# Adding four scan directions and centring them with matmuls, and a grouped convolution over moved copies, in a four-layer vision kernel on one core

## The chip, the core and the metric

The kernel runs on one core of one Trainium2 chip. Five engines work side by side, each through its own instruction queue in order: PE (TensorE, matrix multiplication into PSUM), DVE (VectorE), ACT (ScalarE), POOL (GpSimd) and SP (SyncE, which here issues nearly all DMA transfers). The metric is the device time of one execution in microseconds (us), as the median of several runs. A profile is one further execution with every instruction recorded.

## What is computed

The input is 4 images of 96 channels, 64 by 64. Four layers follow one another, each as x + layer(group_norm(x)): an attention layer (layer 0), a selective scan over four directions with a gated convolution block (layer 1), a 3x3 convolution (layer 2) and a second selective scan with more blocks (layer 3). Two pieces of it matter here. In both scan layers the results of four directions are added and normalised over 192 channels:

```python
# layer 1 (layer 3 has the same with its own names)
ys = (y1 + y2 + y3 + y4).reshape(Bs, E, Hs, Ws)      # E = 192; y3, y4 are transposed in h and w
yn = jnp.moveaxis(ys, 1, -1)
mu = yn.mean(-1, keepdims=True)
var = yn.var(-1, keepdims=True)
yn = (yn - mu) / jnp.sqrt(var + 1e-05) * ln_g + ln_b
```

Layer 3 ends in a block with a grouped 3x3 convolution and a 1x1 convolution of the same 24 channels:

```python
up = conv2d(x[:, :uc], s1)                            # 48 -> 24 channels
low = conv2d(x[:, uc:], s2)
Y1 = conv2d(up, gw, gb, groups=2) + conv2d(up, p1)    # 24 -> 96 channels
Y2 = jnp.concatenate([conv2d(low, p2), low], 1)
```

## The kernel before

The heavy part is eight selective scans: layers 1 and 3 for each of the four images. A scan is cut into 384 units; one unit takes a tile of 128 partitions (16 states times 8 channels) by 1024 positions. For a unit, SP fetches rep (the step sizes, repeated), ACT takes its exponential (L1786), PE spreads the driving term into bx with two bf16 matmuls over 24 rows, DVE multiplies bx by B (L1800) and runs the scan instruction (hs, L1807), POOL multiplies by C (rep, times_c, L1819), and for every third unit PE adds up the states of three units in acc. rep is fetched four units ahead, bx is made two units ahead.

Everything else is written as Python generators, the stages "first" (group norm, layer 0, and the input projection and depthwise convolution of layer 1), "second" (the end of layer 1, layer 2 and the beginning of layer 3) and "third" (the end of layer 3). The program order is written out by hand: scan 0 is accompanied by first(1), scans 1 and 2 by second(0) and second(1), scans 3 and 4 by first(2) and first(3), scans 5 and 6 by second(2) and second(3), and scan 7 by third(0), third(1) and third(2), one after the other. Before scan 0, first(0) runs with nothing beside it; after scan 7, third(3) does (here called the tail).

How much of a stage goes beside a unit is a budget, in slots of about one matmul of 512 columns: each unit gets PACE, less 2.1 in every third unit (where the sums in acc stand), and at most half a slot is carried over. In a unit at most two slots begin, the second one only while more than 0.9 of the budget is left. When a scan nears its end (unit 365), what is left of the stage is run at once.

```python
PACE = 3.5
...
if at == 0:
    work, owed = Slots(beside(s)), 0.0
...
if at == per - NG - LEAD - 1:
    work.run()
owed = min(owed, 0.5) + PACE - (2.1 if i % 3 == 1 else 0.0)
```

second and third begin with directions. For each half h of the 192 channels it loads the row-wise sum (y_row) into V and the column-wise sum (y_col) into yc, of which there is one buffer, and POOL adds yc, read across its rows, to V in eight blocks of 512 (L1370). layer_norm follows: per block, two matmuls with a constant 1/192 form the mean, DVE subtracts it from both halves (L1138), ACT squares the result (L1140), and a matmul with one column set adds the squares into one row of the bank acc. Then come a square root, a reciprocal, and a matmul that spreads each row again.

In third, squeeze makes up (24 channels, padded to 66 by 66) and low (24 channels). The grouped convolution then runs per block of 512 positions as nine matmuls over the 24 rows of up, one for each tap, and a tenth with the 1x1 weights (conv with more); an eleventh, over low, makes Y2. All matmuls go through one helper, line L948 of the profile.

Of the kernel before, what the change touches and what calls it, by code (L numbers as in the profile page):

```python
# [9 lines left out]
F32 = mybir.dt.float32  # L10
# [13 lines left out]
PADW = 66  # L24
# [869 lines left out]
def streams(ctx: ExitStack, tc: tile.TileContext, x, wts, cst, out, wat, cat, flag):  # L894
# [14 lines left out]
    ct = keep.tile([128, n0 + n2 - n1], F32, name="ct")  # L909
    cols = keep.tile([128, 5], F32, name="cols")  # L910
    nc.scalar.dma_start(out=ct[:, :n0], in_=cst[:, :n0])
# [3 lines left out]
    def wv(name, rows=None):  # L915
        return _view(wt, wat[name], rows)
# [16 lines left out]
    addn = cv("addn")  # L933
    for j, v in enumerate((GN_EPS, 1.0, -1.0, 1.0 / 96.0, 1.0 / 192.0)):
# [9 lines left out]
    def img(t):  # L944
        return t.rearrange("p (a b) -> p a b", b=W)
# [134 lines left out]

    def conv(o, weight, src, j, k=3, more=()):


        n = k * k
        taps = [(weight[:, t, :], src[:, 8 * j + t // k : 8 * j + t // k + 8, t % k : t % k + W]) for t in range(n)]
        taps.extend(more)
# [34 lines left out]
    def layer_norm(pool, V, n, gains, each):  # L1121
# [25 lines left out]
        add(7)  # L1147
        yield
        r = pool.tile([8, PCH], F32, name="ln_r", bufs=1)
        nc.scalar.activation(r, acc[:8], AF.Sqrt, bias=eps[:8])  # L1150
# [207 lines left out]
    def directions(pool, b):  # L1358

        V = pool.tile([96, 2, L], F32, name="V", bufs=1)  # L1360
        with tc.tile_pool(name="dirs", bufs=1) as T:
            for h in range(2):
                t = T.tile([96, W, H], F32, name="yc")
                for j in range(4):
                    nc.sync.dma_start(out=t.rearrange("p a b -> p (a b)")[:, bass.ts(j, CH)],
                                      in_=y_col[h][b][:, bass.ts(j, CH)])
                    nc.sync.dma_start(out=V[:, h, bass.ts(j, CH)], in_=y_row[h][b][:, bass.ts(j, CH)])
                for j in range(8):
                    v = img(V[:, h, bass.ts(j, PCH)])
                    nc.gpsimd.tensor_tensor(v, v, t[:, :, 8 * j : 8 * j + 8].rearrange("p a b -> p b a"), ALU.add)  # L1370
# [170 lines left out]
    def finish(PX, b, V):  # L1541
        with tc.tile_pool(name="p3", bufs=2) as pool:
# [15 lines left out]

            yield from layer_norm(pool, V, 2, wv("l3_ss_outn_g"), gate)
            for j in range(8):  # L1560
# [9 lines left out]
        with tc.tile_pool(name="p4", bufs=2) as pool:  # L1570
            up = pool.tile([24, PADW, PADW], F32, name="up", bufs=1)
            border(up, 1)
            low = pool.tile([24, L], F32, name="low", bufs=1)

            def squeeze(j):
                js = bass.ts(j, PCH)
                v = V[:, 0, js]
                nc.scalar.activation(v, v, AF.Identity, bias=wv("l3_ln_b"))
                yield 0.5
                for m, o in enumerate((inner(up, j), img(low[:, js]))):  # L1580
                    q = bank()
# [6 lines left out]
            w = staged(pool, "l3_gwc", "l3_pwc1", "l3_y2", "l3_fin")  # L1588

            sums = pool.tile([96, 2, 8], F32, name="csums", bufs=1)  # L1590
            for j in range(8):
                js = bass.ts(j, PCH)
                p = bank()
                yield from conv(p[:96], w["l3_gwc"][:24], up, j, more=[(w["l3_pwc1"][:24], inner(up, j))])
                nc.scalar.activation(V[:, 0, js], p[:96], AF.Identity, bias=wv("l3_gwc_b"),
                                     accum_out=sums[:, 0, j : j + 1])
                yield 1
                q = bank()
                mm(q[:96], w["l3_y2"][:24], low[:, js])
                yield  # L1600
                nc.scalar.activation(V[:, 1, js], q[:96], AF.Identity, accum_out=sums[:, 1, j : j + 1])
                yield 1
# [258 lines left out]
    store, waiting = [], []  # L1861

# [88 lines left out]
    with tc.manual_schedule():  # L1951
# [83 lines left out]
```

## Time and profile before

| | |
|---|---|
| time, median of 3 runs | 15360.42 us (15356.96 to 15373.58) |
| the profiled execution, its own time | 15373.82 us |
| its span, first to last instruction | 15371.9 us |
| PE busy | 12696.9 us, 83% |
| PE's mean granted clock | 0.799 |
| DVE busy | 11681.2 us, 76% |
| POOL busy | 10373.1 us, 67% |
| ACT busy | 8329.7 us, 54% |
| DMA moved | 2645.47 MB, 172 GB/s over the span |

The profile gives for each group of instructions the busy time, the mean duration of one and the idle time of its engine just before them, with what ended it. Matmuls are pipelined: a record's own duration can be longer than the distance to the next record, so the cost of one in a dense row is the group's busy time over its count. A float32 matmul leaves two records. A tile called one, bx, acc or held is in PSUM; "one" is what a stage works in beside a scan, and the same matmuls stand under "bx" where a stage runs alone.

### The profile page before, as it was taken

What the parts mean: (1) busy time and instruction counts of PE and PEld (TensorE: products, weight loads), DVE (VectorE), ACT (ScalarE), POOL (GpSimd) and SP (SyncE); (2) the same over time, 40 slices, a digit from 0 to 9 for tenths busy, and PEclk for the clock granted to TensorE, in tenths of its full rate; (3) what the DMA queues carried; (4) which work ended last, traced back from release to release, by engine and by line L of the source; (5) the groups of instructions that cost most, each with busy time, mean ns of one, the idle gap of its engine ahead of it and who ended that gap; (6) DMA issues with size and microseconds to landing.
All of it is one profiled execution on the core that took longest, in us unless ns stands there. A gap on an engine that the chain in (4) does not pass through costs nothing.

```text
span 15371.9 us, 128027 instructions
## 1 busy us (share of the span) xinstructions
PE 12696.9 (83%) x41106; PEld 3467.9 (23%) x41106; DVE 11681.2 (76%) x7516; ACT 8329.7 (54%) x11647; POOL 10373.1 (67%) x4722
## 2 busy tenths in 40 slices
PE   8978986988879797888788985988789796868778
PEld 2322221222212121222122221222222121211112
DVE  0067888887879888779877888888888787767771
ACT  3155565556745575555655564656645575444531
POOL 0056777777868677678866877877778676656660
PEclk9977886888879787879778886988889786666655
DMA  0066788786878787768866787787878687666660
GB/s 8 26 155 161 187 201 203 188 202 173 218 175 203 178 201 194 170 165 200 218 156 165 189 205 196 194 199 177 213 179 205 171 208 182 158 156 159 163 157 24
DMA packets 901883, 2645.47 MB, mean 172 GB/s; under 512 B 106640, under 2 KB 256752, under 8 KB 901200
## 3 DMA queue, kind: packets, MB, share of 16 engines
q1 hardware_dynamic: 900544, 2635.94, 69.2%
q8 instruction: 326, 5.34, 0.2%
q14 instruction: 357, 2.92, 0.1%
q10 hardware_dynamic: 656, 1.27, 0.0%
HBM read 2170.18 MB, written 466.62 MB: 172 GB/s over the span
## 4 chain that ended last, share of the span: by engine, by line
PE 48%; DVE 19%; DMA 8%; POOL 7%; ACT 7%; issue 6%; SPq 1%; DVEq 0%; POOLq 0%; another core or an unknown queue 0%; ACTq 0%
PE one L948 30%; DVE hs L1807 13%; PE acc L948 8%; PE bx L948 8%; DVE bx L1800 4%; DMA rep<-dd 4%; POOL rep L1819 4%; PE held L948 2%; ACT rep L1786 2%; POOL V L1370 1%; ACT L1786 1%; ACT ex L1233 1%; DMA yc<-ycol 1%; POOL delta L1731 0%; ACT delta L1726 0%
## 5 line engine op out<-in xcount | busy, mean ns | idle before, releaser
L1819 POOL TENSOR_TENSOR rep<-hs,bc 128x1024 f32<-128x1024 f32 x3072 | 7234.2, 2359 | 3398.4 <-DVE hs L1807 2906.3
L1807 DVE TENSOR_TENSOR_SCAN hs<-rep,carry,bx 128x1024 f32<-128x1024 f32 x2304 | 5401.4, 2344 | 335.6 <-POOL rep L1819 75.4
L1800 DVE TENSOR_TENSOR bx<-bx,bc 128x1024 f32<-128x1024 f32 x3072 | 3721.5, 1211 | 1197.8 <-PE bx L948 1097.4
L1786 ACT ACTIVATE rep<-rep,l_decay 128x1024 f32<-128x1024 f32 x3072 | 3495.8, 1143 | 818.3 <-DMA rep<-dd 790.6
L948 PE MATMUL bx<-parts,spread 24*128 24x512 bf16 x6144 | 1433.7, 438 | 1709.5 <-DVE hs L1807 1662.9
L948 PE MATMUL acc<-rep,ct 128*32 128x512 f32 x12288 | 2628.7, 739 | 165.9 <-POOL rep L1819 165.8
L1807 DVE TENSOR_TENSOR_SCAN hs<-rep,bx 128x1024 f32<-128x1024 f32 x768 | 1754.4, 2284 | 237.1 <-POOL rep L1819 153.2
L948 PEld LDWEIGHTS <-spread 24*128 24x128 bf16 x6144 | 314.2, 93 | 4199.2 <-DVE hs L1807 2774.5
L948 PE MATMUL one<-band,dg 96*96 96x512 f32 x2304 | 1117.1, 620 | 0.0
L948 PE MATMUL one<-upad,diag 96*96 96x512 f32 x2016 | 1033.1, 649 | 4.0 <-ACT ur L1113 2.7
L948 PEld LDWEIGHTS acc<-rep,ct 128*32 128x32 f32 x12288 | 508.7, 127 | 1993.6 <-issue 1513.4
L948 PE MATMUL one<-qq,kk 96*128 96x512 f32 x1152 | 826.6, 807 | 132.4 <-ACT ex L1233 79.0
L1233 ACT ACTIVATE ex<-one 128x512 f32<-128x512 f32 x576 | 343.0, 595 | 758.6 <-PE one L948 753.8
L1786 ACT ACT_TABLE_LOAD x500 | 641.5, 1283 | 96.6 <-DMA rep<-dd 88.4
L948 PE MATMUL one<-pr,ct 6*96 6x512 f32 x1024 | 649.2, 729 | 37.6 <-ACT pr L1691 6.2
L948 PE MATMUL one<-hp,diag 96*96 96x512 f32 x1152 | 618.9, 676 | 51.9 <-POOL diag L1073 51.9
L1815 ACT COPY carry<-hs 128x1 f32<-128x1 f32 x2304 | 408.8, 177 | 398.6 <-DVE hs L1807 395.9
L948 PE MATMUL one<-vpad,diag 96*96 96x512 f32 x1200 | 598.6, 635 | 0.0
L948 PE MATMUL held<-ex,cols 128*32 128x256 f32 x3072 | 571.8, 453 | 12.0 <-ACT ex L1233 6.0
L948 PE MATMUL held<-ex,vT 128*32 128x256 f32 x3072 | 572.3, 453 | 0.0
L948 PEld LDWEIGHTS one<-band,dg 96*96 96x96 f32 x2304 | 350.0, 166 | 531.3 <-issue 515.7
L948 PEld LDWEIGHTS one<-upad,diag 96*96 96x96 f32 x2016 | 321.4, 174 | 500.7 <-issue 483.6
(3395 smaller groups left out, 14517.9 us busy)
## 6 DMA issues: line engine op xcount, KB each, us to landing
rep<-dd SPq DMA_DIRECT2D x3072, 512.0 KB
parts<-du SPq DMA_DIRECT2D x1024, 144.0 KB
bc<-rows SPq DMA_DIRECT2D x256, 512.0 KB
dd<-delta SPq DMA_DIRECT2D x256, 384.0 KB
du<-cut SPq DMA_DIRECT2D x256, 384.0 KB
us<-urow SPq DMA_DIRECT2D x128, 384.0 KB
du<-cut SPq DMA_DIRECT2D x256, 192.0 KB
yrow<-yo SPq DMA_DIRECT2D x128, 384.0 KB
```

Source lines behind the costliest of these rows:

```text
L948: nc.tensor.matmul(o, lhsT=lhsT, rhs=rhs, start=first, stop=last)
L1233: nc.scalar.activation(last.rearrange("p a b -> p (a b)"), p, AF.Exp, scale=HD**-0.5)
L1370: nc.gpsimd.tensor_tensor(v, v, t[:, :, 8 * j : 8 * j + 8].rearrange("p a b -> p b a"), ALU.add)
L1786: nc.scalar.activation(a, a, AF.Exp, scale=decay[tag][:, k, NG * h + m : NG * h + m + 1])
L1800: nc.vector.tensor_mul(bx, bx, ready[i // NG][2][:, 0, :])
L1807: nc.vector.tensor_tensor_scan(out=hs, data0=a, data1=bx, initial=carry[:, h, m : m + 1] if c else 0.0, op0=ALU.mult, op1=ALU.add)
L1815: nc.scalar.copy(carry[:, h, m : m + 1], live[i][1][:, CH - 1 : CH])
L1819: nc.gpsimd.tensor_tensor(a, hs, ready[i // NG][2][:, 1, :], ALU.mult)
```

## The change

Three things are changed.

- The sum and the centring. directions loads both halves of yc before it begins (two buffers) and y_row in blocks of 512, one block ahead. For each block and half, four matmuls add up in one bank: the two parts of the same half with the matrix centre, and the two parts of the other half with a constant -1/192. The yc parts are read across rows, at a stride of 64 elements. ACT copies the bank to V. centred takes the place of layer_norm's first part and only squares and adds; scaled is layer_norm's second part, unchanged.
- The grouped convolution. up becomes 96 partitions by 66 by 64: three copies of the 24 channels at partitions 0, 32 and 64, moved by one column each. The weights stand beneath one another in gw, the 1x1 weights are added to the middle tap by POOL, and three matmuls over 96 rows take the place of ten over 24. sq3 makes the three copies in one matmul, and ACT writes them in three parts.
- The order. PACE is 3.65, and a stage begins at unit 2 of its scan, not at unit 0.

```diff
-    def conv(o, weight, src, j, k=3, more=()):
+    def conv(o, weight, src, j, k=3):
...
+    minus_mean = cols[:, 5:6].to_broadcast([128, 96])
+    centre = keep.tile([96, 96], F32, name="centre")
+    nc.vector.tensor_scalar(centre, ident[:96, :96], 1.0 / 192.0, None, ALU.subtract)
...
+    def centred(pool, V, gains, each):
+        acc = held()
+        sq = []
+        def add(last):
+            k, t = sq.pop()
+            mm(acc[:8], cv("means")[:96, 1, 7 - k // 2 : 15 - k // 2], t, k == 0, last)
+        for k in range(16):
+            if sq:
+                add(False)
+                yield
+            t = pool.tile([96, PCH], F32, name="ln_sq", bufs=2)
+            nc.scalar.activation(t, V[:, k % 2, bass.ts(k // 2, PCH)], AF.Square)
+            sq.append((k, t))
+            yield 0
+        add(True)
+        yield
+        yield from scaled(pool, V, 2, gains, each, acc)
...
     def directions(pool, b):
         V = pool.tile([96, 2, L], F32, name="V", bufs=1)
         with tc.tile_pool(name="dirs", bufs=1) as T:
+            yc = [T.tile([96, W, H], F32, name=f"yc{h}") for h in range(2)]
+            def rows(j):
+                t = T.tile([96, 2, PCH], F32, name="yr", bufs=2)
+                for h in range(2):
+                    nc.sync.dma_start(out=t[:, h, :], in_=y_row[h][b][:, bass.ts(j, PCH)])
+                return t
+            yr = rows(0)
             for h in range(2):
-                t = T.tile([96, W, H], F32, name="yc")
                 for j in range(4):
-                    nc.sync.dma_start(out=t.rearrange("p a b -> p (a b)")[:, bass.ts(j, CH)],
+                    nc.sync.dma_start(out=yc[h].rearrange("p a b -> p (a b)")[:, bass.ts(j, CH)],
                                       in_=y_col[h][b][:, bass.ts(j, CH)])
-                    nc.sync.dma_start(out=V[:, h, bass.ts(j, CH)], in_=y_row[h][b][:, bass.ts(j, CH)])
-                for j in range(8):
-                    v = img(V[:, h, bass.ts(j, PCH)])
-                    nc.gpsimd.tensor_tensor(v, v, t[:, :, 8 * j : 8 * j + 8].rearrange("p a b -> p b a"), ALU.add)
+            for j in range(8):
+                ahead = rows(j + 1) if j < 7 else None
+                for h in range(2):
+                    p = bank()
+                    parts = [(m, v) for k, m in ((h, centre[:96]), (1 - h, minus_mean[:96])) for v in
+                             (img(yr[:, k, :]), yc[k][:, :, 8 * j : 8 * j + 8].rearrange("p a b -> p b a"))]
+                    for t, (m, v) in enumerate(parts):
+                        mm(p[:96], m, v, t == 0, t == 3)
+                        if t < 3:
+                            yield (1,)
+                    yield
+                    nc.scalar.copy(V[:, h, bass.ts(j, PCH)], p[:96])
                     yield 1
+                yr = ahead
...
-                yield from layer_norm(pool, V, 2, wv("l1_ln_g"), gate)
+                yield from centred(pool, V, wv("l1_ln_g"), gate)
...
-            up = pool.tile([24, PADW, PADW], F32, name="up", bufs=1)
-            border(up, 1)
+            up = pool.tile([96, PADW, W], F32, name="up", bufs=1)
+            for s in (up[:, 0, :], up[:, PADW - 1, :], up[0:32, :, 0:1], up[64:96, :, W - 1 : W]):
+                nc.gpsimd.memset(s, 0.0)
+            sq3 = pool.tile([96, 3, 32], F32, name="sq3", bufs=1)
+            nc.gpsimd.memset(sq3, 0.0)
+            gw = pool.tile([96, 3, C], F32, name="gw", bufs=1)
+            nc.gpsimd.memset(gw, 0.0)
+            pw = pool.tile([96, C], F32, name="pw", bufs=1)
+            n, m, _ = wat["l3_gwc"]
+            for s in range(3):
+                nc.gpsimd.tensor_copy(sq3[:, s, 0:24], wv("l3_sq")[:, 0, :])
+                nc.sync.dma_start(out=gw[32 * s : 32 * s + 24],
+                                  in_=wts[:24, n : n + m].rearrange("p (a b c) -> p a b c", a=3, b=3)[:, :, s, :])
+            n, m, _ = wat["l3_pwc1"]
+            nc.sync.dma_start(out=pw[32:56], in_=wts[:24, n : n + m])
+            nc.gpsimd.tensor_tensor(gw[32:56, 1, :], gw[32:56, 1, :], pw[32:56], ALU.add)
...
-                for m, o in enumerate((inner(up, j), img(low[:, js]))):
-                    q = bank()
-                    mm(q[:24], wv("l3_sq")[:, m, :], v)
-                    yield
-                    nc.scalar.copy(o, img(q[:24]))
-                    yield 1
+                q = bank()
+                mm(q[:96], sq3.rearrange("p a b -> p (a b)"), v)
+                yield
+                for s in range(3):
+                    a, n = max(1 - s, 0), W - abs(1 - s)
+                    nc.scalar.copy(up[bass.ts(s, 32), 1 + 8 * j : 9 + 8 * j, a : a + n],
+                                   img(q[bass.ts(s, 32)])[:, :, a + s - 1 : a + s - 1 + n])
+                yield 1
+                q = bank()
+                mm(q[:24], wv("l3_sq")[:, 1, :], v)
+                yield
+                nc.scalar.copy(low[:, js], q[:24])
+                yield 1
...
-                yield from conv(p[:96], w["l3_gwc"][:24], up, j, more=[(w["l3_pwc1"][:24], inner(up, j))])
+                for t in range(3):
+                    mm(p[:96], gw[:, t, :], up[:, 8 * j + t : 8 * j + t + 8, :], t == 0, t == 2)
+                    if t < 2:
+                        yield (1,)
+                yield
...
-    PACE = 3.5
+    PACE = 3.65
...
             if at == 0:
+                work = idle
+            if at == 2:
                 work, owed = Slots(beside(s)), 0.0
```

More of the change, by code (lines that the diff above doesn't have):

```diff
@@ L909, in streams @@
     ct = keep.tile([128, n0 + n2 - n1], F32, name="ct")
-    cols = keep.tile([128, 5], F32, name="cols")
+    cols = keep.tile([128, 6], F32, name="cols")
     nc.scalar.dma_start(out=ct[:, :n0], in_=cst[:, :n0])
@@ L933, in streams @@
     addn = cv("addn")
-    for j, v in enumerate((GN_EPS, 1.0, -1.0, 1.0 / 96.0, 1.0 / 192.0)):
+    for j, v in enumerate((GN_EPS, 1.0, -1.0, 1.0 / 96.0, 1.0 / 192.0, -1.0 / 192.0)):
         nc.gpsimd.memset(cols[:, j : j + 1], v)
@@ L1079, in diagonals @@
         return d
-    def conv(o, weight, src, j, k=3, more=()):
+    def conv(o, weight, src, j, k=3):
         n = k * k
         taps = [(weight[:, t, :], src[:, 8 * j + t // k : 8 * j + t // k + 8, t % k : t % k + W]) for t in range(n)]
-        taps.extend(more)
         for t, (lhsT, rhs) in enumerate(taps):
@@ L1148, in layer_norm, with scaled @@
         yield
+        yield from scaled(pool, V, n, gains, each, acc)
+    def centred(pool, V, gains, each):
[15 more added lines that the diff above has]
+        yield from scaled(pool, V, 2, gains, each, acc)
+    def scaled(pool, V, n, gains, each, acc):
         r = pool.tile([8, PCH], F32, name="ln_r", bufs=1)
@@ L1557, in gate @@
                     yield 1
-            yield from layer_norm(pool, V, 2, wv("l3_ss_outn_g"), gate)
+            yield from centred(pool, V, wv("l3_ss_outn_g"), gate)
             for j in range(8):
@@ L1579, in squeeze @@
                 yield 0.5
-                for m, o in enumerate((inner(up, j), img(low[:, js]))):
-                    q = bank()
-                    mm(q[:24], wv("l3_sq")[:, m, :], v)
-                    yield
-                    nc.scalar.copy(o, img(q[:24]))
-                    yield 1
+                q = bank()
[11 more added lines that the diff above has]
+                yield 1
             yield from layer_norm(pool, V[:, 0:1, :], 1, wv("l3_ln_g"), squeeze)
-            w = staged(pool, "l3_gwc", "l3_pwc1", "l3_y2", "l3_fin")
+            w = staged(pool, "l3_y2", "l3_fin")
             sums = pool.tile([96, 2, 8], F32, name="csums", bufs=1)
@@ L1857, in streams @@
     AHEAD, BEHIND, LEAD = 4, 2, 6
-    PACE = 3.5
+    PACE = 3.65
     total = len(groups) * NG
     per = total // len(SCANS)
-    store, waiting = [], []
+    store, waiting, owed = [], [], 0.0
     def later(n, f):
```

## The prediction

> **What bounds the kernel now.** I read the chain of waits first, then the busy time in windows, then the groups by shape, then the timeline of the tail.
>
> ```profile
> PE 48%; DVE 19%; DMA 8%; POOL 7%; ACT 7%; issue 6%; SPq 1%; DVEq 0%; POOLq 0%; another core or an unknown queue 0%; ACTq 0%
> PEclk9977886888879787879778886988889786666655
> ```
>
> PE carries half of the chain, and it is granted only 0.6 of its clock in the last seventh of the span. To place that, I counted off the 3072 scan instructions (hs, L1807) in eights of 384 units: scans 0 to 7 start at 829, 2548, 4242, 5972, 7687, 9408, 11103 and 12827 us, the tail at 14979. Seven scans take 1693 to 1731 us; scan 7, which has three "third" stages beside it, takes 2152; the tail, the fourth "third" with nothing beside it, takes 393. Then windows of 24 units; columns: length, then busy us and count for PE, PEld, DVE, ACT, POOL, then PE clock, DMA share, GB/s:
>
> ```profile
> 1071.60:1187.80 116.20, 104.83 (x508) 26.98 (x504) 89.52 (x55) 68.72 (x109) 77.17 (x34) 0.81 0.67 164
> 2452.90:2548.10 95.20, 49.19 (x160) 8.54 (x160) 85.42 (x51) 44.17 (x48) 78.05 (x35) 0.55 0.83 202
> 2912.00:3004.60 92.60, 91.55 (x295) 27.43 (x294) 83.96 (x49) 58.52 (x72) 79.15 (x35) 0.96 0.83 197
> 13352.10:13510.50 158.40, 122.06 (x270) 31.76 (x268) 97.33 (x67) 55.34 (x90) 73.70 (x32) 0.60 0.58 145
> 14978.80:15371.90 393.10, 333.00 (x448) 88.86 (x448) 66.47 (x95) 57.45 (x104) 22.59 (x19) 0.60 0.09 24
> ```
>
> In order: attention beside a scan; a scan with its side stage finished; the dense band convolution; the third's grouped convolution; the tail. A scan unit has a floor of about 3.87 us (95.2/24 and 92.6/24), set by VectorE (85 busy of 92 to 95). The scan's own PE work is 49.19 x 0.55 / 24 = 1.13 us a unit at full clock. Where PE is dense it holds the clock (0.96), and a unit stays at the floor; where the grouped convolution runs, the clock is 0.60 and a unit takes 6.6 us. The groups say why:
>
> ```profile
> L948 PE MATMUL bx<-up,l_gwc 24*96 24x512 f32 x144 | 126.3, 1058 | 0.0
> L948 PE MATMUL bx<-upad,diag 96*96 96x512 f32 x288 | 125.3, 594 | 0.0
> L1106 ACT COPY upad<-one 96x512 f32<-96x512 f32 x112 | 63.3, 580 | 70.1 <-PE one L948 69.6
> L1114 ACT COPY uc<-ur 96x512 f32<-96x512 f32 x128 | 140.6, 1099 | 4.1
> L1370 POOL TENSOR_TENSOR V<-V,yc 96x512 f32<-96x512 f32 x128 | 193.7, 1522 | 178.3 <-DMA yc<-ycol 131.8 <-DMA V<-yrow 33.9 <-issue 12.7
> ```
>
> Both convolutions run gap-free outside the scans. With 24 rows in, a record costs 126.3/144 = 0.877 us; with 96 rows 125.3/288 = 0.435. A float32 matmul of 512 columns leaves two records, so 1.75 us against 0.87.
>
> **What the Trainium skill says.** "TensorE: Matmul & The Clock Gate", Part 1, gives PE two speeds, half by default and full after sustained activity; the factor of 2.0 between the two rows above agrees, and so does the clock following PE's density. The same page, "Why this matters for your kernels", says that a matmul over 32 rows takes as long as one over 128; here 24 rows are even slower, because of the clock. "SBUF — State Buffer", "Door 1: The DMA port swizzle", says that reads that go to a new 16-byte line each time pay a penalty. The trace agrees for ScalarE: the copy that reads at a stride of 64 elements takes 1099 ns, the plain one 580, 1.9 times. No TensorE read at such a stride is in this trace, and the change makes 32 per direction call.
>
> **The change, part by part.** Where each section falls I take from the built changed program's instruction order, which shows no time.
>
> *Tail (393 us).* Before, the grouped convolution runs from 15183.7 to 15333.8, 150 us: 8 blocks x (10 + 1) matmuls x 1.71. After: 8 x (3 + 1) x 0.87 = 28 at full clock, taken as 36 for evictions: -114. Against that, the directions. Before, the second half's data are there at 14998.1 and Sqrt's table load comes at 15034.7: 37 us for POOL's last adds and the centring. After, 64 matmuls stand there: 32 plain x 0.87, and 32 that read yc across rows, which I bound by 0.87 (no penalty) and 3.5 (four times); I take ScalarE's ratio, 0.87 x 1.9 = 1.64. 28 + 52 + 16 squares x 0.87 = 94: +57. The sixteen evictions by ScalarE (0.58) and the squares hide behind PE, since ScalarE is 85% idle here. Two more copies per block in squeeze (2 x 0.58), half hidden: +5. Sum -52.
>
> *Third, three times beside scan 7.* First third before, by section, in us (units): directions and centring 141 (22), gate 90 (15), out projection and second norm 79 (15), squeeze 101 (23), grouped convolution 191 (34), end 82 (11): 684 in 120. After: directions 64 matmuls (80) + squares (14) + 36 x 1.13 = 135 of PE, under the DVE floor of 36 x 3.87 = 139; the loads come first: yr 0 and 1 and both yc, 3.9 MB at about 220 GB/s = 18 us, during which PE, in order, holds back the scan's bx and so VectorE, less the two units that are ahead: +13. With some idle clock, 170. The loads before stalled POOL twice (17 and 15 us from issue to first add in scan 1), so this is a stall moved from POOL to PE, not a new one. The stage now begins at unit 2 of a scan, with the last y store issued just ahead of it; on SP's queue one yc load waits for that store's landing (some 3 us), with rep fetches behind it, again inside the 4 units. Gate 80, projection 70, squeeze 92 (same work in fewer units), convolution 32 x 0.87 + 14 x 1.13 = 44, under its floor of 54, taken as 60; end 72. Sum 544 in about 103 units: -140 each, -420. The stages now end at unit 308, not 356: 48 more bare units x 3.87 = +186. The setup on POOL (memsets, and an add that waits for the gw and pw loads, with times_c queued behind it) I put at 5 us each, +15. SP's gw loads wait for those memsets, with rep fetches behind them; those are issued 4 units ahead, which covers it. Sum -220.
>
> *Second, four times.* Directions and centring: 22 units in 135 us become 36 in 170, +35. VectorE loses 16 subtractions of 0.68, which hid in its waits: nothing. Pace 3.65 packs the rest: bands 138 units in 555 us become 127 x 3.98, -50; later convolutions, 11 units fewer, about 3 us each, -33; the burst that closes the scan at unit 365 (a 17 us unit, with the remaining work run at once) goes, as the stage ends at 354, -13; bare units 19 become 30, +43. About -20 each, between +20 and -60; -80.
>
> *First, three times.* Untouched but for pace: the built order shows two slots in every unit, where the collecting unit had one; attention's 144 units become 122, and the stage ends at unit 305, not 341. PE's work there at full clock is the windows' busy time times clock: 498 of 707 us, a share of 0.70; 162 of it are the scan's. After, 336 + 122 x 1.13 = 474. At the old share that takes 677 us; the bands reach 0.95. Denser work should keep the clock: I take 0.80, 592, -115. The later convolutions are at the floor, 14 units fewer x 3.88 = -54; bare units +36 x 3.87 = +139. -30 each, between +55 (0.70) and -95 (0.90); -90.
>
> *Whole.* -52 - 220 - 80 - 90 = -442. The profiled execution took 15373.8 us (span 15371.9), 13 above the median of 15360.4. So 14932 there, 14920 as a median. Head (829 us) unchanged: the setup's few small instructions lie beside its loads.
>
> **Rivals.**
> 1. *The clock doesn't answer to packing* (18%). Attention stays at 0.70 (+165 for three), seconds gain nothing, third and tail as above: -107, about 15250. For it: the attention windows show 0.81 with PE already 90% busy. Against: the bands' 0.96 at 99% busy.
> 2. *Strided reads are free and PE stays warm* (17%). The tail's directions lose another 25 us, the seven beside scans some 10 each, attention goes to 0.90 (another 195): about -730, so 14630 at the far end. For it: float32 needs a new element only each 0.83 ns (0.427 us a record over 512). Against: ScalarE, at 1.13 ns (580/512), already pays 1.9 times.
> 3. *Slower: the strided reads* (9%). PE becomes the bound of every direction call: 8 x 32 = 256 strided matmuls, all on PE's queue with the scan's bx and acc behind them. The saving of 442 is gone at 442/256 = 1.73 us more each, that is at 3.4 us a matmul (3.9 times plain). At 4 us: +604 - 442 = +162, about 15520. For it: nothing shows PE's read at this stride. Against: POOL's strided add takes 1.52 us, ScalarE's copy 1.9 times plain.
> 4. *The new convolution stays cold* (inside my range). If 96 rows with 1 in 4 matmuls still of 24 rows get half clock, the tail gains 28 less, each third about 20.
>
> **Numbers.** Forecast as summed: 56%, 14780 to 15080. A measurement tells apart about 0.2%, 31 us. Faster 0.88 (forecast, rivals 1 and 2, less a little), same 0.03, slower 0.09. Range 14690 to 15250: it leaves out rival 3 and the far ends of 1 and 2.
>
> **What would show it.** Right: in the tail, up,gw records near 0.44 us apart and the convolution under 45 us; scan 7 near 1930 us; attention windows at clock 0.85 or more; the POOL row of V gone; PE waiting for yc once per call. Wrong: yr records much shorter than yc records beyond 1.9 times; attention clock still 0.8 (then scans 0, 3 and 4 are longer than 1720); directions over 200 us in scans 1, 2, 5 and 6.

## The result, and the profile after

| | before | after |
|---|---|---|
| time, median (4 runs each) | 15367.0 us | 15167.8 us (15149.9 to 15176.1) |
| ratio, with its 95% interval | | 0.9867 (0.985 to 0.9884) |
| span of the profiled execution | 15371.9 us | 15158.0 us |
| PE's mean granted clock | 0.799 | 0.826 |

The change gains about 200 us, 1.3%, where 440 were forecast. The direction and the range were right (15168 lies inside 14690 to 15250), the size was not.

First the place. I counted off the scan instructions (hs) in eights again, as the prediction did for the kernel before:

| stage | before | after | change | forecast |
|---|---|---|---|---|
| head | 829 | 818 | -11 | 0 |
| scans 0, 3, 4 (beside "first"), sum | 5156 | 5169 | +13 | -90 |
| scans 1, 2, 5, 6 (beside "second"), sum | 6843 | 6835 | -8 | -80 |
| scan 7 (beside three "thirds") | 2152 | 1998 | -154 | -220 |
| tail | 393 | 337 | -56 | -52 |

The tail's sum came out as worked out, scan 7 gave two thirds of what was forecast, and the seven other scans gave nothing. These stage times come from one profiled execution of each kernel; in the kernels of this document that leave scans 0, 3 and 4 as they were, their sum varies between 5143 and 5156, so a few us in a stage mean nothing.

The busy share and the clock over the span, from the page of the kernel after (40 equal slices; each digit is a tenth):

```profile
PE   8978986988979797888768885988979787787858
PEclk9978986888979887889778896897979888777767
```

In the last seven slices, where the thirds and the grouped convolution stand, 0.6 to 0.8 of the clock is granted now and 0.5 to 0.6 was before. The windows of the kernel after answer to those of before. Columns: stretch, length, then busy us and count for PE, PEld, DVE, ACT, POOL, then PE clock, DMA share, GB/s:

```profile
1063.60:1189.50 125.90, 110.78 (x574) 28.73 (x570) 88.00 (x51) 71.94 (x116) 78.51 (x34) 0.86 0.59 148
2271.70:2360.50 88.80, 47.75 (x160) 8.53 (x160) 85.41 (x51) 50.62 (x76) 77.41 (x35) 0.60 0.93 225
2544.00:2674.10 130.10, 113.40 (x273) 26.50 (x274) 84.50 (x50) 52.82 (x84) 79.67 (x35) 0.82 0.72 186
2902.40:2995.10 92.70, 92.34 (x304) 27.44 (x302) 83.84 (x49) 54.38 (x64) 76.88 (x34) 1.00 0.82 201
14821.40:15158.00 336.60, 289.39 (x429) 69.02 (x428) 56.31 (x79) 76.04 (x136) 1.83 (x10) 0.73 0.10 30
```

In order: attention; bare units; the directions of scan 1 (its first 24 units); the bands; the tail. The bare units and the bands are at the floor (88.8 and 92.7 us for 24 units). Attention is denser and is granted 0.86, as the prediction wanted, but its 24 units now take 125.9 us where they took 116.2: more side work in each. The tail's clock rose from 0.60 to 0.73. In scan 7 the grouped convolution takes, from its first matmul to its last, 56, 53 and 47 us where it took 189, 183 and 197, and the three thirds end 1711 us after the scan's start, 570 each against the 544 forecast. What is new is the third window: 24 units take 130 us, and **PE is busy for 113 of them while DVE is busy for 84.5**. Most of the other 17 us PE waits for loads (below). In that stretch PE is the bound and not DVE.

What PE does there is told apart by the timeline of the tail, where the same matmuls run with nothing beside them. PE, by start and length in us; x2 is one matmul, of two records:

```profile
14834.96 1.89 PE L951 MATMUL bx<-yr,centre 96*96 96x512 f32 x2
14836.64 1.90 PE L951 MATMUL bx<-yc,centre 96*96 96x512 f32 x2
14838.37 1.04 PE L951 MATMUL bx<-yr,cols 96*96 96x512 f32 x2
14839.24 1.87 PE L951 MATMUL bx<-yc,cols 96*96 96x512 f32 x2
14840.94 1.04 PE L951 MATMUL bx<-yr,centre 96*96 96x512 f32 x2
```

The distance from one start to the next is the cost. In the trace the granted clock goes from half to full at 14836.9. The first plain matmul (yr) lies before that: 1.68 us. Later a plain one costs 0.87, but the one that reads yc across its rows costs 14840.94 - 14839.24 = 1.70. The rest of the trace shows the strided read at half clock too. Of the matmuls of yr and yc that are followed by another without a gap and lie wholly in one state of the clock, a plain one costs 0.94 us at full clock (median of 185) and 1.81 at half (26), a strided one 1.80 at full (196) and 1.81 at half (41). The strided read does not follow the clock. The records beside the scans, where the clock changes all the time, say the same (min/median/max in ns):

```profile
L951 PE MATMUL one<-yc,centre x224: 1017/1033/1168, 2564.9 to 14102.0; 96*96 96x512 f32 x112
L951 PE MATMUL one<-yr,cols x224: 590/608/1061, 2566.7 to 14103.4; 96*96 96x512 f32 x112
```

A plain record is short at full clock and long at half; the strided one is always long.

The load wait is where the prediction put it, once per call. PE's timeline at unit 3 of scan 1 (start, length, operation, idle time before):

```profile
2550.48 0.61 PE L951 MATMUL bx<-parts,spread 24*128 24x512 bf16 x2
2557.16 1.99 PE L951 MATMUL one<-yr,centre 96*96 96x512 f32 x2 [6.08 <-issue]
2564.91 1.99 PE L951 MATMUL one<-yc,centre 96*96 96x512 f32 x2 [5.76 <-DMA yc<-ycol]
2566.72 1.89 PE L951 MATMUL one<-yr,cols 96*96 96x512 f32 x2
2571.10 1.99 PE L951 MATMUL one<-yc,cols 96*96 96x512 f32 x2 [2.49 <-DMA yc<-ycol]
2573.02 0.61 PE L951 MATMUL bx<-parts,spread 24*128 24x512 bf16 x2
```

6.08 + 5.76 + 2.49 = 14 us idle, and the scan's own next bx matmul, at 2573.02, stands behind them. For the first 6.08 the profile names no cause ("issue"); that it is the load of yr is an inference, which e8 below supports: with the loads given time, no idle time is left before these yr matmuls.

### The profile page after: what moved, and what is told of

The parts are those of the page before. It is cut to its first block, busy times and chain, and to the rows that moved or that the text cites. A ratio compares the mean times of both kernels' runs of the same rounds, so it can differ in the third digit from the quotient of the medians.

```text
span 15158.0 us, 128823 instructions
## 1 busy us (share of the span) xinstructions
PE 12567.7 (83%) x41426; PEld 3424.4 (23%) x41426; DVE 11624.3 (77%) x7389; ACT 8424.4 (56%) x11840; POOL 10198.5 (67%) x4619
## 5 line engine op out<-in xcount | busy, mean ns | idle before, releaser
L951 PE MATMUL acc<-rep,ct 128*32 128x512 f32 x12288 | 2553.2, 732 | 5.0 <-POOL rep L1890 4.9
L951 PE MATMUL one<-qq,kk 96*128 96x512 f32 x1152 | 744.0, 732 | 141.3 <-ACT ex L1260 85.4
L1857 ACT ACT_TABLE_LOAD x503 | 645.3, 1283 | 92.9 <-DMA rep<-dd 84.5
L951 PE MATMUL held<-ex,cols 128*32 128x256 f32 x3072 | 529.1, 422 | 6.7
L951 PE MATMUL held<-ex,vT 128*32 128x256 f32 x3072 | 529.6, 422 | 0.0
```

The source lines that it names most:

```text
L951: nc.tensor.matmul(o, lhsT=lhsT, rhs=rhs, start=first, stop=last)
L1857: nc.scalar.activation(a, a, AF.Exp, scale=decay[tag][:, k, NG * h + m : NG * h + m + 1])
```

## Experiments

What is open after this reading is which part of the change gave what, why the seven scans gained nothing, and whether the strided read, the wait or the pace is to blame. All times are medians of four runs, all ratios are to the kernel before as it ran beside them. PACE is 3.5 in the kernels built on the one before, unless said otherwise.

### 1. The parts of the change alone

**e1_after_pace35**: the whole change but for the pace.

```diff
-    PACE = 3.65
+    PACE = 3.5
```

> The changed kernel with PACE back at 3.5, all else as changed. Theory A (packing is worth nothing: what the denser units save, the bare units at the end of a scan give back): within 30 us of the changed kernel, so 15140 to 15200; scans 0, 3 and 4 again 1715 to 1725 us. Theory B (3.65 costs: the bare units are a loss): 15060 to 15110, scans 0, 3, 4 unchanged and 1, 2, 5, 6 shorter. Theory C, the prediction's (3.65 gains some 170): 15280 to 15340.

Measured: 15176.2 us, ratio 0.9876 (0.9853 to 0.9899). The pace is worth 8 us on the changed kernel, which is nothing beside the 31 us that can be told apart: Theory A. By stages, taking 3.65 instead of 3.5 gave: scans 0, 3, 4 +9, seconds -74, scan 7 +39, tail +14. So the packing does help the seconds, which at 3.5 end in a burst; here is the window over the last 24 units of scan 1 with pace 3.5, 141 us where the floor is 93:

```profile
4111.40:4252.40 141.00, 95.88 (x276) 26.45 (x274) 85.79 (x51) 65.09 (x68) 77.05 (x34) 0.75 0.64 163
```

But scan 7, whose thirds follow one another and need no last-minute burst, loses half of what the seconds win. The tail, in which the pace plays no part, is longer for another reason, told in section 3.

**e4_before_pace365**: the kernel before with only the pace.

```diff
-    PACE = 3.5
+    PACE = 3.65
```

> The kernel before with PACE 3.65 alone. Theory A: within 40 us of the kernel before. Theory B: slower by 60 to 100 us. Theory C, the prediction's: faster by 120 to 200 us (scans 0, 3, 4 by 30 each, 1, 2, 5, 6 by 15 to 20, scan 7 by some 20).

Measured: 15470.6 us, ratio 1.006 (1.0036 to 1.0084): slower by 103, a little more than Theory B's 60 to 100. Scan 7 is 46 us longer, and scans 3, 4 and 5 by 16 to 21 each. In attention the clock did rise with the packing, from 0.81 to 0.89; the window over its 24 units:

```profile
1083.30:1202.50 119.20, 107.41 (x574) 28.23 (x570) 87.74 (x51) 71.83 (x116) 78.55 (x34) 0.89 0.64 156
```

The expectation that followed the prediction is refuted: a denser PE is granted more clock, and the scan still gets no shorter.

**e2_conv_only**: the kernel before with the moved copies and three matmuls over 96 rows (up, sq3 and gw as in the change), nothing else. Of the edit, the loop over the blocks:

```diff
-                yield from conv(p[:96], w["l3_gwc"][:24], up, j, more=[(w["l3_pwc1"][:24], inner(up, j))])
+                for t in range(3):
+                    mm(p[:96], gw[:, t, :], up[:, 8 * j + t : 8 * j + t + 8, :], t == 0, t == 2)
+                    if t < 2:
+                        yield (1,)
+                yield
```

> The kernel before with the moved copies and the three-matmul convolution alone; directions, layer_norm and PACE 3.5 as before. Theory A (the convolution is all of the gain and the directions cost some of it): scan 7 about 1970, tail about 290, in all 15050 to 15110, faster than the whole change. Theory D (the directions gain too, by taking work off POOL): 15180 to 15250, slower than the whole change.

Measured: 15096.6 us, ratio 0.9824 (0.9802 to 0.9846): -271; in the profiled execution all of it lies where thirds run (scan 7 -168, tail -114). As Theory A had it, this part alone is faster than the whole change.

**e3_dirs_only**: the kernel before with the new directions and centring and the start at unit 2 (centre is made in each call), old convolution.

> The kernel before with the directions and the centring by TensorE alone (the matrix centre is made anew by one small VectorE operation in each call, for lack of room), stage from unit 2, PACE 3.5, grouped convolution as before. Theory A: tail +57, each scan with directions +10 to +20 at its beginning: 15460 to 15560. Theory D: 15270 to 15350.

Measured: 15526.2 us, ratio 1.0099 (1.0076 to 1.0121): +158. Every stage but the head is as long as before or longer: seconds +43 in sum, scans 0, 3, 4 +48, scan 7 +45, tail +48. The 48 of scans 0, 3 and 4 can't be a cost of the directions' matmuls, for none stands there; the start at unit 2, or chance in the one profiled execution (24 us above the median), remain, and no run here separates them.

The whole is therefore, step by step from before: convolution -271 (e2), directions on top of it 15176.2 - 15096.6 = +80 (e1), pace on top of both -8. The parts do not simply add: directions cost 158 beside the old convolution and 80 beside the new one, and the pace, -8 here, costs 103 on the kernel before.

### 2. Why the directions cost time

**e5_plain_read**: the changed kernel, with yc read in its own order. It leaves out the transposition of the column-wise directions.

```diff
-    (img(yr[:, k, :]), yc[k][:, :, 8 * j : 8 * j + 8].rearrange("p a b -> p b a"))
+    (img(yr[:, k, :]), yc[k][:, 8 * j : 8 * j + 8, :])
```

> The changed kernel with yc read in its own order (512 consecutive elements) in place of across its rows; so the column-wise directions are added untransposed, and the rest is unchanged. It prices the stride by itself. Theory A (32 strided matmuls a call at 1.70 us against 0.87 are on the path wherever PE is the bound): tail 27 us shorter, seven calls beside scans 10 to 20 each, in all 14990 to 15070. Rival (beside scans the stride hides under VectorE's floor): only the tail, 15130 to 15150.

Measured: 14897.9 us, ratio 0.9701 (0.9685 to 0.9718): 270 us below the changed kernel, more than either theory had. The gain lies where the directions run: the four seconds -129 in sum, scan 7 -88, tail -39; scans 0, 3, 4, which have no directions, -9. Its window over the first 24 units of scan 1, with the columns as above:

```profile
2535.20:2637.30 102.10, 90.45 (x274) 25.66 (x275) 83.46 (x49) 53.35 (x84) 78.16 (x35) 0.87 0.96 238
```

And the group of the tail that reads yc (busy us, mean ns of one | idle before), first of the changed kernel, then of e5:

```profile
L951 PE MATMUL bx<-yc,centre 96*96 96x512 f32 x32 | 30.2, 1031 | 0.0
L951 PE MATMUL bx<-yc,centre 96*96 96x512 f32 x32 | 16.8, 605 | 0.0
```

PE's busy time falls from 113.4 to 90.5 us for the same number of matmuls, and the stretch from 130 to 102. In the tail the busy time of this group is 30.2 us in the changed kernel and 16.8 here. Summed over the four groups that read yc, the stride costs PE 191 us in 256 matmuls (beside scans 423.8 - 258.6, in the tail 60.2 - 34.8); the other 79 of the 270 come on top of the work itself. Parts of them are no effect of the stride. In the tail the grouped convolution takes 35 us here and 48 in the changed kernel, because the full clock came earlier: 13. Scans 0, 3 and 4 give 9. And a block of yc in its own order lies in one of the four loads of a half, a block across the rows in all four, so the edit also shortens a wait: PE's idle time for yc beside the scans falls from 59 to 26 us. What these 33 are worth isn't known; e8 takes away more of such waiting for little gain.

**e8_loads_ahead**: the changed kernel, with 12 slots given to nothing between the issue of the loads and the first matmul, so that PE does not wait.

```diff
+            yield 12
             for j in range(8):
                 ahead = rows(j + 1) if j < 7 else None
```

> The changed kernel with 12 slots put between the loads and the first matmul of directions, so that PE doesn't stand in front of yc with the scan's bx behind it. If PE's wait (16 us at unit 3 of scan 1) is lost time: 10 to 14 us less in each of seven calls, 15070 to 15110. If the loads hold back the rep fetches as well: 15150 to 15190.

Measured: 15139.7 us, ratio 0.9851 (0.9835 to 0.9868): -28. It falls between what the two theories had. PE's idle time before the matmuls of yr and yc beside the scans falls from 107 to 13 us, so the wait is real, but to take it away is worth a tenth of what e5 gains. (28 us is about the least that can be told apart; the four times of e8 all lie below the four of the changed kernel.)

**e9_act_turns**: ScalarE copies each block of yc into order once, and both matmuls that read it read the copy. All of the computation is there.

```diff
+                yt = T.tile([96, 2, PCH], F32, name="yt", bufs=2)
+                for k in range(2):
+                    nc.scalar.copy(img(yt[:, k, :]), yc[k][:, :, 8 * j : 8 * j + 8].rearrange("p a b -> p b a"))
+                yield 1
...
-                    (img(yr[:, k, :]), yc[k][:, :, 8 * j : 8 * j + 8].rearrange("p a b -> p b a"))
+                    (yr[:, k, :], yt[:, k, :])
```

> The changed kernel, but ScalarE first copies each block of yc, read across its rows, into a small tile in order (two copies a block of j, 1.1 us each), and the matmuls read that. All outputs stay as they should. Theory A (the stride costs because PE is the bound of a directions call; ScalarE, 56% busy, has room for it): close to e5_plain_read, 14890 to 14970. Rival S (ScalarE's exponentials of the scan stand behind the copies): 15000 to 15110.

Measured: 14973.0 us, ratio 0.9747 (0.9731 to 0.9763): -195 against the changed kernel, most of what e5 gains, and 3 us above Theory A's range. It adds 128 copies of 1.04 us, to an engine that is busy for little more than half of the span.

**e12_act_turns_ahead**: e9 with e8's pause.

```diff
+            yield 12
             for j in range(8):
```

> e9_act_turns with the 12 slots between loads and first matmul of e8_loads_ahead. Theory A: another 20 to 40 us less than e9_act_turns. Rival: nothing, as then the pace is what ends the call.

Measured: 14880.0 us, ratio 0.9691 (0.9669 to 0.9712), the fastest of all and the version to take: 487 below the kernel before, 288 below the changed one. Against e2, which has the old directions, it is 217 below: with the blocks turned first and the loads given time, the new directions, with the pace and start that go with them, do pay. The pause gains 93 here, where 20 to 40 were expected, and only 28 in e8. With the copies on ScalarE it is ScalarE, which also makes each unit's exponential, that stands still for the loads, 208.7 us in all, and 46.2 with the pause. The group of these copies in e9 (the time after the bar is ScalarE's idle time before them):

```profile
L1407 ACT COPY yt<-yc 96x512 f32<-96x512 f32 x128 | 132.6, 1080 | 208.7 <-DMA yc<-ycol 208.7
```

The same group in e12:

```profile
L1408 ACT COPY yt<-yc 96x512 f32<-96x512 f32 x128 | 132.6, 1081 | 46.2 <-DMA yc<-ycol 46.2
```

The window over the first 24 units of scan 1 in e12 takes 105 us. PE is busy for 82 of them (with 241 records where the changed kernel had 273, as the directions begin later), no more than VectorE's 83:

```profile
2543.00:2647.70 104.70, 82.05 (x241) 21.59 (x242) 83.20 (x50) 60.60 (x90) 79.49 (x35) 0.77 0.91 229
```

**e10_pool_adds**: POOL adds yc to yr as it did before, and PE only centres, with two matmuls per block and half instead of four.

```diff
+                for k in range(2):
+                    v = img(yr[:, k, :])
+                    nc.gpsimd.tensor_tensor(v, v, yc[k][:, :, 8 * j : 8 * j + 8].rearrange("p a b -> p b a"), ALU.add)
+                yield 1
...
-                    for t, (m, v) in enumerate(parts):
-                        mm(p[:96], m, v, t == 0, t == 3)
-                        if t < 3:
+                    for t, (k, m) in enumerate(((h, centre[:96]), (1 - h, minus_mean[:96]))):
+                        mm(p[:96], m, yr[:, k, :], t == 0, t == 1)
+                        if t < 1:
```

> The changed kernel, but POOL adds yc to yr as before the change (1.52 us, two a block), and two matmuls over the sums take the place of four. Theory A: PE has 32 plain matmuls a call, 28 us, a quarter of the changed kernel's 82; POOL's work comes back: 14880 to 14980, faster than e2_conv_only. Rival P (POOL in order in front of times_c is the bound of a call): 15050 to 15150, like e2_conv_only.

Measured: 15106.0 us, ratio 0.9831 (0.981 to 0.9852): -62 against the changed kernel, but +133 against e9; Rival P had it. (28 us of PE's 82, in the expectation, is a third and not a quarter.) The directions have half the matmuls of the changed kernel, and PE waits for the adds instead, as this kernel's group shows:

```profile
L951 PE MATMUL one<-yr,centre 96*96 96x512 f32 x224 | 173.6, 868 | 165.8 <-POOL yr L1407 149.9 <-DMA yc<-ycol 11.3 <-DMA rep<-dd 4.5
```

POOL also multiplies every unit's states by C, and in the program's order each add of 1.5 us stands among those. It matters which engine turns the block.

**e7_pool_two_yc**: e2 with the old directions, but two buffers of yc, a start at unit 2 and the 12 slots' pause before POOL's adds, so that POOL need not wait for loads.

> The convolution alone (as in e2_conv_only, directions on POOL, PACE 3.5), with both halves of yc and V loaded at once into their own buffers at unit 2 and the first add put off by 12 slots. If POOL's two waits for loads (17 and 15 us in scan 1 before, once per half) are on the path: some 15 to 20 us less for each of seven calls, 14960 to 15010. If the wait only moves (rep fetches queued behind the loads): 15080 to 15120.

Measured: 15153.5 us, ratio 0.9864 (0.9848 to 0.9881), which neither theory had: 57 us slower than e2. The wait did go; POOL's adds were preceded by 154.8 us of idle time for yc in e2 and by 11.4 here (group of e7):

```profile
L1373 POOL TENSOR_TENSOR V<-V,yc 96x512 f32<-96x512 f32 x128 | 193.9, 1524 | 11.4 <-DMA yc<-ycol 11.4
```

Taking away POOL's idle time ahead of these adds did not make the kernel faster. What costs the 57 us stays open; the three edits came together, and seven of the eight scans became longer, by 1 to 26 us. Scans 0, 3 and 4, which have no adds of yc, give 34 of it.

### 3. Rows or count in the grouped convolution

**e6_ten_over_96**: e2, but ten matmuls over the 96 rows instead of three (the taps are repeated, so the sum holds them several times).

```diff
-                for t in range(3):
-                    mm(p[:96], gw[:, t, :], up[:, 8 * j + t : 8 * j + t + 8, :], t == 0, t == 2)
+                for t in range(10):
+                    mm(p[:96], gw[:, t % 3, :], up[:, 8 * j + t % 3 : 8 * j + t % 3 + 8, :], t == 0, t == 9)
-                    if t < 2:
+                    if t < 9:
```

> The convolution alone as in e2_conv_only, but with ten matmuls over the 96 rows in place of three (each of the three repeated, so the sum holds taps several times): the old count with the new number of rows. Theory R (the rows set the clock, half of the gain is the clock): in the tail the convolution takes 8 x 11 x 0.87 = 77 us (150 before, 33 in e2_conv_only), scan 7 about 2080, in all 15180 to 15260. Rival N (the count is all, the clock stays): tail and scan 7 as before, 15340 to 15400.

Measured: 15141.4 us, ratio 0.9854 (0.9837 to 0.987): -224 with the same count of matmuls as before, more than Theory R had.

**e11_three_over_24**: e2, but its three matmuls read the first 24 rows only, so two of the three copies are left out of the sum.

```diff
-                    mm(p[:96], gw[:, t, :], up[:, 8 * j + t : 8 * j + t + 8, :], t == 0, t == 2)
+                    mm(p[:96], gw[:24, t, :], up[:24, 8 * j + t : 8 * j + t + 8, :], t == 0, t == 2)
```

> As e2_conv_only, but each of the three matmuls reads only the first 24 rows, so two of three copies are left out of the sum: few matmuls, few rows. With before (ten, 24), e6_ten_over_96 (ten, 96) and e2_conv_only (three, 96) it completes the square. Theory R (rows set the clock, count the rest): half clock again, the tail's convolution 8 x 4 x 1.71 = 55 us, in all 15110 to 15150. Theory N2 (with so few matmuls the clock hardly matters): 15090 to 15110.

Measured: 15151.6 us, ratio 0.9861 (0.9845 to 0.9877): -215, 2 us above Theory R's range. The group of the convolution's records in the tail, first of e6:

```profile
L948 PE MATMUL bx<-up,gw 96*96 96x512 f32 x160 | 71.9, 604 | 0.0
```

The same group of e11:

```profile
L948 PE MATMUL bx<-up,gw 24*96 24x512 f32 x48 | 43.0, 1061 | 0.0
```

And of e2:

```profile
L948 PE MATMUL bx<-up,gw 96*96 96x512 f32 x48 | 24.0, 634 | 0.0
```

A record takes 71.9/160 = 0.449 over 96 rows, 43.0/48 = 0.896 over 24, though both run without a gap. That the clock is what differs is seen in the windows from the first matmul of the tail's grouped convolution to the last, with the columns as above. In order: before, e11, e6, e2, and the changed kernel:

```profile
15180.00:15333.80 153.80, 152.84 (x179) 48.37 (x178) 0.00 (x0) 12.14 (x32) 0.00 (x0) 0.50 0.00 0
15047.00:15105.20 58.20, 57.27 (x67) 17.11 (x66) 0.00 (x0) 13.27 (x34) 0.00 (x0) 0.50 0.00 0
15022.80:15105.30 82.50, 81.07 (x179) 27.65 (x177) 0.00 (x0) 13.29 (x34) 0.00 (x0) 0.99 0.00 0
15017.60:15052.10 34.50, 33.10 (x67) 9.40 (x65) 0.00 (x0) 13.27 (x34) 0.00 (x0) 0.96 0.00 0
15072.30:15120.00 47.70, 46.55 (x67) 12.16 (x65) 0.00 (x0) 13.26 (x34) 0.00 (x0) 0.68 0.00 1
```

PE is equally dense in all five. Over 24 rows it stays at 0.50; over 96 it goes to full. But it need not go there at once: full clock comes 2 to 3 us after the first of these matmuls in e6 and e2, and 31 us after it in the changed kernel. Of the seven other kernels with three matmuls over 96 rows, traced once each, five took 35 us for this stretch and two (e8, e10) 48 to 51. Why the clock comes late in some is open. It is also behind 13 of the 14 us by which the tail of e1 is shorter than that of the changed kernel.

The square of whole times:

| us | 24 rows | 96 rows |
|---|---|---|
| ten matmuls | 15367 (before) | 15141 (e6) |
| three matmuls | 15152 (e11) | 15097 (e2) |

Either remedy alone gives 215 to 226 us, both together some 270: filling the rows doubles the speed of each matmul once the full clock is there, having three instead of ten divides what is left to speed up.

## Why the prediction was right in part

To set the sum against the runs I regroup its terms by part, each as time above the floor of 3.87 us a unit, so that units which only move to another section cancel:

| part | forecast | measured |
|---|---|---|
| convolution: tail -114 + 5; thirds (191 - 34 x 3.87) - (60 - 14 x 3.87) = 54 each | -270 | -271 (e2) |
| directions: tail +57; seconds (135 - 22 x 3.87) - (170 - 36 x 3.87) = 19 each; thirds 25 each | -95 | +80 (e1 against e2) |
| pace: scans 0, 3, 4 | -90 | -8 (after against e1) |
| setup +15 and small remainders | +13 | not separated |

**Right: the convolution.** Its mechanism (few rows, half the clock) and its size both hold; e6 and e11 separate rows from count. In the tail, 36 us were taken for the convolution with Y2; it is 24.0 + 8.7 = 33 in e2, and 34.0 + 11.5 = 45.5 in the changed kernel, where the clock stayed at half for the first 31 us: rival 4, in part. So "under 45 us" was just missed, and "up,gw records near 0.44 us apart" is 0.71 in the changed kernel and 0.50 in e2. That the tail's sum was met (-56 against -52) owes something to luck: from the scan's end to the Sqrt load it is 49 us longer (+57 forecast), the convolution, which took 154 us before and not 150, is 106 shorter (-114 forecast), and two misses cancel. The Trainium skill, "TensorE: Matmul & The Clock Gate", "Why this matters for your kernels", says that a matmul over 32 rows takes as long as one over 128. At half clock this case agrees (2 x 0.877 = 1.75 us over 24 rows, 1.68 over 96); e11 against e2, 0.896 to 0.50 us a record at the same count and columns, shows that it holds at one clock only, and that the rows help to decide which clock it is.

**Right: the stride's price on PE.** The prediction took 1.64 us for a strided matmul against 0.87, which is 0.77 x 256 = 197 us of PE in all. Measured: 1.70 against 0.87 from start to start, and 191 in all by e5. The figure was borrowed from ScalarE's ratio of 1.9, so that it held is in part luck: at half clock, where strided and plain both cost 1.81, the ratio is 1.0, which the prediction did not foresee.

**The failing step: "135 of PE, under the DVE floor of 36 x 3.87 = 139".** The sum spread PE's work in a direction call over 36 units. But the matmuls that read yr and yc stand in units 4 to 26; the nine units that follow only square and add. For 27 units the same figures give 80 + 27 x 1.13 = 111 of PE against a floor of 104: PE is the bound there even at full clock, while 0.82 was granted, and a slower read lies on the path. Measured, in the first 24 units of scan 1, PE is busy for 113 of 130 us and waits for loads in 14 more, and DVE is busy for 84.5. The section until unit 36, for which 170 had been taken, took 189 to 192 in scans 1, 2, 5, 6 and 7; with plain reads it is 157 to 161. So the stride cost some 30 us in each of seven calls, where the prediction had let it cost 10 (the seven calls of its rival 2). In the tail, where 25 had been taken, e5 gives 39, of which 13 are the clock of the grouped convolution. The "+13" a call for the loads was no part of the miss: taking the wait away in e8 is worth 28 us for all eight calls together.

The directions' row in the table is off by 175. That is not the stride's work alone: by stages e1 is 63 us longer than e2 in the seconds and 44 in the tail, but 26 shorter in scan 7, and in the seconds pace 3.5 ends in a burst, of which pace 3.65 takes 74 us back. How the cost divides between directions and pace depends on the order in which they are added.

**The second failing step: "Denser work should keep the clock: I take 0.80".** The share of PE's full clock used in attention (busy x clock over length) rose from 0.70 to 0.76 only. In the prediction's own sum that is 474/0.76 = 624 us in place of 592, 32 more in each scan, and each was to gain 30. Measured from its first exponential to its last, attention became 73 us shorter (710 to 637, mean of scans 0, 3 and 4) and takes 21 units fewer, which must be run elsewhere: at the floor 21 x 3.87 = 81 us. Scans 0, 3 and 4 are the same at both paces in the changed kernel (5160 and 5169), and on the kernel before the pace costs 103. Packing moves side work to earlier units, and each unit that it empties is run bare later at 3.7 to 3.9 us; what is left as a gain is what the clock adds in the dense part, and that was small.

**The rivals.** Rival 1 came nearest with 15250. Its reason was half right: packing brought nothing in scans 0, 3 and 4, but not because the clock did not answer (attention 0.81 to 0.86, and 0.89 in e4). For the same reason the sign "attention clock still 0.8 (then scans 0, 3 and 4 are longer than 1720)" misleads: the clock rose, and these scans took 1726, 1723 and 1721. Rival 2's argument, that PE needs a new element only each 0.83 ns (the records of before show 0.429 us over 512, 0.84), falls with the 1.70 us. Rival 3 had the right mechanism, PE as the bound of every direction call, and the wrong point at which it decides: 3.4 us a matmul came from setting the stride against a saving of 442 us, of which 95 were to come from these same directions and 90 from the pace. At 1.70 us the directions already cost time (+158 in e3, +80 in e1 against e2); only the convolution kept the whole change on the faster side.

**The parts that were read off the built order held**: thirds that end at unit 308, bands packed into fewer units (from about 550 us to 510 in scan 1, forecast -50), the Sqrt load in the tail 95 us after the data (94 forecast), the wait for loads moved to PE once per call.

**Left open.** The 11 us in the head, where nothing was forecast; what is left of the 79 us by which e5 gains more than the stride's own PE time; the 57 us of e7; why full clock comes late in some tails; why directions cost 158 us beside the old convolution and 80 beside the new one.

## What to carry to other kernels

Before costing work at nothing because its sum over a section lies under another engine's floor, look at the densest window of that section: if the work comes in one run, that run has its own bound. Turn a block once, on an engine with room and a queue that can wait (here ScalarE, with the loads given time to land), rather than have TensorE read it across rows in every matmul: the same block read twice by two halves pays twice. Where an operand fills only a fraction of the rows, stacking shifted copies can pay even if the count of matmuls stays as it is (224 us here); and the pace at which side work is packed is to be measured, as here its gain in one stage was the loss in the next.

## What the hardware showed that I had not expected

- A float32 matmul of 512 columns whose moving operand is read at a stride of 64 elements costs 1.70 us at full clock in the tail, against 0.87 for a plain one. Beside the scans the medians are 1.80 against 0.94 at full clock and 1.81 against 1.81 at half. The penalty is a factor of two at full clock and about nothing at half.
- Matmuls over 24 rows, back to back without a gap, stay at half clock (0.877 before, 0.896 in e11); ten over 96 rows in the same place run at full (0.449 in e6). Three over 96 rows with a fourth over 24 rows reach it too, after 3 us in e2 and after 31 in the changed kernel. Being busy in time was not enough to get the full clock.
